# Two Gram matrices, an attention and 64 units on one core: turning x in 32x32 blocks on VectorE from quartered loads

## The chip, the core and the metric

One NeuronCore of a Trainium2 chip runs the kernel. TensorE (PE) multiplies matrices and writes to PSUM; VectorE (DVE), ScalarE (ACT) and GpSimd (POOL) compute elementwise; SyncE (SP) issues most DMAs. Each engine works through its own instructions strictly in order, and they meet through semaphores. The metric is the device time of the whole kernel in microseconds, from several runs, of which the median counts. All data is fp32.

## What is computed

x has the shape (16, 32, 128, 128). Two layers are added to it in turn, each fed with a group norm `_gn` of its input:

```python
x = x + _L0_conv_ref(_gn(x), Wq, Wkv, Wout, bout)
x = x + _L1_conv_ref(_gn(x), pn_g, pn_b, k1_..., k2_..., k3_..., k4_...)
```

Layer 0 is an attention between channels. The 16 images form two halves of 8 images x 32 channels = 256 rows of 16384 pixels each. q, k and v are linear in these rows, and the scores are summed over the pixels:

```python
sim = jnp.einsum('bin,bjn->bij', qh, kh) * scale
attn = jax.nn.softmax(sim, axis=-1)
out = jnp.einsum('bnj,bjd->bnd', attn, vh)
```

So for each half the scores follow from the 256x256 Gram matrix of the rows (x times x transposed, summed over 16384 pixels) and the row sums, and the whole layer becomes one 256x256 matrix that is applied to x. Layer 1 cuts the image into 8x8 windows and puts four small networks in each (`_fastkan`: a layer norm, eight Gaussians of each normalized value, a linear map of them, and a silu branch).

## The kernel before

The kernel has two stages: a head that makes the layer-0 matrix of each half, and a loop over 64 units (32 per half; a unit is 128 channels x 1024 pixels).

The head. `gram_load` fetches x in 32 loads of 1 MiB (128 partitions, rows of 4 KB) into three `u` tiles. `gram_turn` takes 512 pixels at a time: eight TensorE transposes (L616) into a PSUM tile `Y`, then one ScalarE copy (L624) into one of two `R` tiles, which puts the pixels on the partitions. `gram_sum` multiplies each step's 512 pixels with themselves in strips of 32 channels (L644), 64 matmuls a step, and sums 32 steps into one PSUM tile `X` for a half; only the strips on and above the diagonal blocks are computed. `attention(bp)` is a chain of some forty small steps that go to and fro between TensorE, VectorE and ScalarE, each through a `Y`: means, covariance (`rank_one` adds a rank-one matrix to the sum in `X` by L715; `gram_to` mirrors it), scores, softmax, the matrix `pts[bp]`, and the statistics for the second group norm. `X` is given back after the second `gram_to`. `projections` holds five tiles (two `z`, `ad_r`, two `u`) with the weights of layer 0 from the start until the second attention's end.

The loop. A unit passes through `load` (1 MiB of x, for two units), `layer0_norm` (L953 applies the matrix, L967 centres, L933 gets the variances), `keep`, `rows_norm` (L1000, L1005 to L1013), `move` (eight DMAs, L1046), `silus`, `norm_a` and `norm_b` (L415 into `Y`, L1063, L1066, L933 to L936, L1071), `scale_a`/`scale_b` (L1088), `seed_a`/`seed_b` (L1097 to L1105: four ScalarE activations into a `u` and two `R`), `ladder_a`/`ladder_b` (seven VectorE products each, L1117), `products_a`/`products_b` (L415 and L1153, L1272 into two `X`), `evict_a`, `move_back` (eight DMAs, L1189), `evict_z`, `result`, `again` and `store` (four DMAs of 32 partitions each, L1308).

The order. All tasks are Python generators that ask for steps (an engine, a length in us, tiles). `Flow.run` plans while the program is built: at each turn it picks, of the steps that could begin, the one that begins first by its own reckoning, and emits it. The order on each engine is thus fixed at build time; on the chip an engine waits at an instruction whose inputs aren't there. For the tasks of the loop the order on each engine is written out by hand in `ORDER` (task.step.behind: in slot m the unit m - behind), one period for a unit. Tasks that aren't named in it (the Gram tasks, projections, parameters and attention) go ahead of a named step on the same engine when they could begin no later. Tiles come from pools with a fixed number of buffers, and a step that finds none free can't be picked. Numbers of buffers that matter here: `Y` 2, `X` 2, `R` 3, `u` 6, `z` 2, `sz` 2, `yy` 2, `n` 2, `x`, `ad`, `ad_r` and `d` 1.

Of the kernel before, what the change touches and what calls it, by code (L numbers as in the profile page):

```python
# [46 lines left out]
LANDING = 2.5  # L47
BACK = 2
# [24 lines left out]
}  # L73
TURNS = 7
# [8 lines left out]
class Flow:  # L83
# [56 lines left out]
    def run(self, tasks, units):  # L140
# [32 lines left out]
        while True:  # L173
# [19 lines left out]
            found = []  # L193
            for engine, order in orders.items():
                while heads[engine] < len(order):
                    name, unit, k = order[heads[engine]]
                    x = where.get((name, unit))
                    if unit < 0 or unit >= units or (name, unit) in passed or (x is not None and x["at"][2] > k):
                        heads[engine] += 1
                        continue  # L200
                    break
                else:
                    continue
                head = next((c for c in able if c[1] is x and c[1]["at"][2] == k and c[1]["asks"][0] == engine), None)
                if head is not None:
                    found.append(head)
            free = [c for c in able if c[1]["at"][0] not in named]
            due = {c[1]["asks"][0]: c[0] for c in found}
            free = [c for c in free if c[0] <= due.get(c[1]["asks"][0], c[0])]
            for c in free:  # L210
                found = [d for d in found if d[1]["asks"][0] != c[1]["asks"][0]]
            at, x = min(found + free or able, key=lambda c: c[0])
# [7 lines left out]
def conv_preact_kernel(  # L220
# [34 lines left out]
    x_raw = x.rearrange("b c h w -> (b c) (h w)").rearrange("(k q p) n -> k p q n", q=KK, p=P)  # L255
    out_rows = out.rearrange("b c h w -> (b c) (h w)").rearrange(
# [166 lines left out]
    def layers():  # L423
        with ExitStack() as es:
# [12 lines left out]
                    "n": (sb, narrow, 2),  # L437
# [6 lines left out]
                    "ad": (sb, [P, 8, 2, P], 1),  # L444
                    "ad_r": (sb, [P, 8, 2, P], 1),
# [120 lines left out]
            NX = 3  # L566

            def projections():

                wq, wk, vo, low, mid = yield step("POOL", 5.0, "z", "z", "ad_r", "u", "u")  # L570
                vo = vo.rearrange("p l t w -> p (l t w)")
                wq = wq.rearrange("p (k n) -> p k n", k=KK)
                wk = wk.rearrange("p (k n) -> p k n", k=KK)
                wv_ = low[:, 0:1024].rearrange("p (h k c) -> p h k c", h=PAIRS, k=KK)
                wv_raw = vo[:, 0:1024].rearrange("p (h m s) -> p h m s", h=PAIRS * KK, s=2)
                wo = vo[:, 1024:2048].rearrange("p (h n) -> p h n", h=PAIRS)
# [9 lines left out]

            def gram_load():
                for m in range(NBP * NRB):
                    if m == 0:
                        xs = yield step("SP", 1.6, *["u"] * NX)  # L590
                    else:
                        if m >= NX:
                            yield "get", ("turned", 2 * (m - NX) + 1)
                        yield step("SP", 1.6)
                    bp, j = divmod(m, NRB)
                    t = xs[m % NX].rearrange("p (k n) -> p k n", k=KK)
                    nc.sync.dma_start(out=t, in_=x_raw[bp, :, :, j * RB : (j + 1) * RB])
                    put(("xs", m), t, fl.moved(2.6))

            STEPS = S // 512  # L600

            def gram_turn():
# [6 lines left out]
                for m in range(NBP * STEPS):  # L609
                    xr = yield "get", ("xs", m // 2)  # L610
                    o = (m % 2) * 512
                    tr, = yield step("PE", 0.95, "Y")
# [15 lines left out]
            def gram_sum():  # L628
# [5 lines left out]
                for m in range(NBP * STEPS):  # L634
                    bp, i = divmod(m, STEPS)
                    t = yield "get", ("xT", m)
                    for b in range(4):
                        got = yield step("PE", 0.55, *(["X"] if i == b == 0 else []), lag=0.0)
                        if got:
                            g = got[0]  # L640
# [796 lines left out]
```

## Time and profile before

| | us |
|---|---|
| median of 3 runs | 2930.34 (2930.0 to 2930.73) |
| the profiled execution | 2929.84 |
| its span, first to last instruction | 2927.8 |
| first Gram sum (L644) starts | 10.2 |
| first half's Gram matrix is read (L764) | 117.6 |
| second half's Gram matrix is read (L764) | 240.8 |
| first matmul of a unit's layer 0 (L953) | 240.6 |
| last step of the second attention (L921) | 300.3 |

The profile names engines by the abbreviations above (PEld is TensorE's loading of weights, which overlaps its matmuls), lines as L and a number, and tiles by their names without buffer numbers; a name can be that of the pool's tile, not of what lies in it, so that a line reading `u<-X` at L764 is the attention reading its Gram matrix. An fp32 matmul shows as two records. A time in front is us from the start of the span. The loads of x to the Gram stage are 32 of 1024 KB each, those of the loop another 32.

### The profile page before, as it was taken

To read this page: it belongs to the slowest core of one execution; us is meant where nothing else is said; L and a number is where in the kernel's file an instruction comes from. 1 tells how busy PE (TensorE), PEld (TensorE's weight loads), DVE (VectorE), ACT (ScalarE), POOL (GpSimd) and SP (SyncE) were. 2 spreads that over 40 slices of the span, in tenths; PEclk is the share of its full clock that TensorE was granted. 3 is DMA by queue.
4 is the path that set the end of the run, shared out by engine and by line. 5 is a ranking of instruction groups with operands and counts; after the bars stand their busy time and mean duration, and the time that the engine had idled before them with its cause. 6 is when DMAs were issued, how large, how long until landed. Compare 5 with 4: busy or idle time off the path is not lost.

```text
span 2927.8 us, 105440 instructions
## 1 busy us (share of the span) xinstructions
PE 2808.8 (96%) x48543; PEld 1138.2 (39%) x48543; DVE 2596.7 (89%) x1669; ACT 2578.1 (88%) x2089; POOL 53.6 (2%) x109
## 2 busy tenths in 40 slices
PE   8998899999999999999999999999999999999975
PEld 7885233333333333333333333333333333333321
DVE  1112699999999999999999999999999999999986
ACT  2222899999999999999999999999999999999973
POOL 7000000000000000000000000000000000000000
PEclk9998799999999999999999999999999999999998
DMA  6541223333433333443334343333344333334311
GB/s 206 172 126 63 58 72 112 103 109 112 116 106 107 108 105 113 113 113 91 110 103 109 113 115 110 103 112 105 111 113 114 96 104 105 108 113 114 97 56 39
DMA packets 196440, 311.33 MB, mean 106 GB/s; under 512 B 22944, under 2 KB 154528, under 8 KB 196000
## 3 DMA queue, kind: packets, MB, share of 16 engines
q1 hardware_dynamic: 192000, 302.07, 36.0%
q8 instruction: 382, 6.26, 0.9%
q0 software_dynamic: 3712, 2.46, 0.4%
q14 instruction: 58, 0.48, 0.1%
q10 hardware_dynamic: 288, 0.07, 0.0%
HBM read 103.18 MB, written 67.11 MB: 58 GB/s over the span
## 4 chain that ended last, share of the span: by engine, by line
PE 68%; DVE 21%; issue 6%; ACT 3%; DMA 1%; DVEq 0%; ACTq 0%; SPq 0%
PE X L415 24%; DVE u L1117 15%; PE X L1153 10%; PE Y L953 8%; PE X L644 5%; PE Y L415 4%; PE Y L967 4%; PE X L1272 4%; DVE yc L1088 3%; DVE yy L1005 2%; PE Y L933 2%; PE Y L616 2%; PE Y L1071 2%; ACT R L1099 0%; ACT u L1097 0%
## 5 line engine op out<-in xcount | busy, mean ns | idle before, releaser
L1117 DVE SCALAR_TENSOR_TENSOR u<-R,u 128x2048 f32<-128x2048 f32 x910 | 2042.5, 2286 | 33.8 <-ACT u L1102 17.0
L415 PE MATMUL X<-u,wt_a 32*32 32x512 f32 x16384 | 658.0, 601 | 8.7 <-ACT u L1102 4.2
L415 PE MATMUL X<-u,wt_b 32*32 32x512 f32 x16896 | 635.9, 602 | 18.2 <-ACT u L1102 9.3
L415 PEld LDWEIGHTS X<-u,wt_a 32*32 32x32 f32 x16384 | 302.8, 103 | 285.1 <-issue 134.4
L415 PEld LDWEIGHTS X<-u,wt_b 32*32 32x32 f32 x16896 | 224.5, 103 | 385.8 <-issue 196.5
L1088 DVE TENSOR_TENSOR yc<-yc,Y 128x1024 f32<-128x1024 f32 x260 | 305.4, 1216 | 13.1 <-PE Y L1071 9.8
L1097 ACT ACTIVATE u<-yc,vec 128x2048 f32<-128x2048 f32 x130 | 258.5, 1988 | 25.8 <-DVE yc L1088 21.2
L953 PE MATMUL Y<-x,pt 128*128 128x512 f32 x512 | 240.4, 613 | 34.0 <-DVE yc L1088 33.2
L1105 ACT ACTIVATE R<-yc,vec 128x2048 f32<-128x2048 f32 x130 | 259.5, 1996 | 2.1 <-DVE u L1117 1.2
L1099 ACT ACTIVATE R<-yc,vec 128x2048 f32<-128x2048 f32 x130 | 258.7, 1990 | 0.0
L1063 ACT ACTIVATE yc<-Y 128x1024 f32<-128x1024 f32 x260 | 250.4, 1017 | 8.3 <-PE Y L415 8.3
L1066 ACT ACTIVATE u<-yc 128x2048 f32<-128x2048 f32 x130 | 247.6, 1905 | 3.3 <-DVE u L1117 2.5
L1102 ACT ACTIVATE u<-u 128x2048 f32<-128x2048 f32 x130 | 247.1, 1901 | 0.0
L624 ACT COPY R<-Y 128x1024 f32<-128x1024 f32 x64 | 64.9, 1013 | 161.4 <-PE X L644 151.2
L935 ACT ACTIVATE lr<-Y,vec 128x512 f32<-128x512 f32 (+1 forms) x194 | 131.5, 678 | 39.0 <-PE Y L933 38.9
L953 PEld LDWEIGHTS Y<-x,pt 128*128 128x128 f32 x512 | 93.4, 192 | 184.4 <-issue 94.0
L644 PE MATMUL X<-R 128*32 128x161 f32 (+7 forms) x4096 | 146.0, 291 | 3.5 <-issue 3.4
L933 PE MATMUL Y<-u,e 128*32 128x512 f32 x1040 | 141.2, 608 | 5.0 <-ACT u L1066 5.0
L644 PEld LDWEIGHTS X<-R 128*32 128x32 f32 x4096 | 127.9, 110 | 24.5 <-issue 17.0
L1181 ACT ACTIVATE ad<-X,col 128x1024 f32<-128x1024 f32 x128 | 134.1, 1097 | 0.0
L967 PE MATMUL Y<-xh,c 128*128 128x512 f32 x256 | 128.8, 626 | 2.5 <-DVE yc L1088 1.4
L936 ACT ACTIVATE lr<-lr 128x512 f32<-128x512 f32 (+1 forms) x194 | 122.4, 631 | 6.2
(197 smaller groups left out, 2644.7 us busy)
## 6 DMA issues: line engine op xcount, KB each, us to landing
xh<-xh SPq DMA_DIRECT2D x128, 512.0 KB
d<-yy SPq DMA_DIRECT2D x512, 128.0 KB
ad_r<-ad SPq DMA_DIRECT2D x512, 128.0 KB
u<-in_x SPq DMA_DIRECT2D x32, 1024.0 KB
x<-in_x SPq DMA_DIRECT2D x32, 1024.0 KB
out<-xh SPq DMA_DIRECT2D x256, 128.0 KB
col<-in_cols POOLq DMA_DIRECT2D x32, 0.5 KB, 4.8
sz<-in_w POOLq DMA_DIRECT2D x32, 4.5 KB, 4.7
```

The costliest lines, as they stand in the source:

```text
L415: MM(dst(to, g_), lhsT=wt[32 * g_ : 32 * g_ + 32, :], rhs=rhs(g_, (to - turn[g_]) % 4), start=start, stop=stop,)
L644: MM(g[32 * q : 32 * q + 32, k, lo:hi], lhsT=t[:, b, at : at + 32], rhs=t[:, b, lo:hi], start=first, stop=last,)
L953: MM(xp[:, u, :], lhsT=pts[bp][:, k, kk * P : (kk + 1) * P], rhs=xr[:, k, u * 512 : (u + 1) * 512], start=k == 0, stop=k == KK - 1,)
L1063: ACT(v[:, i * RB : (i + 1) * RB], flat(yt[i]), AF.Identity)
L1066: ACT(sq, v, AF.Square)
L1088: TT(v[:, o], v[:, o], flat(rb[i]), ALU.mult)
L1097: ACT(u, v, AF.Square, bias=bq)
L1099: ACT(up, v, AF.Exp, bias=bp_, scale=2.0)
L1102: ACT(u, u, AF.Exp, scale=-1.0)
L1105: ACT(down, v, AF.Exp, bias=bn, scale=-2.0)
L1117: STT(t, by, BIG, tiles[at[way]], ALU.min, ALU.mult)
L1153: MM(dst(i, f), lhsT=wt(i)[o, o], rhs=rhs(i, o), start=False, stop=False)
```

## The change

- **Loads.** x comes to the Gram stage in 16 loads of 2 MiB (2048 pixels of 256 rows), each in eight DMAs: for each of two blocks of 128 rows and each quarter of the pixels, 32 channels go to 32 partitions, with four images side by side on a partition, in rows of 2 KB. The two buffers are made of `ad`, a `yy` and two `u` instead of three `u`. A load waits until the one two before has been turned.
- **Turning.** Two VectorE transposes (128x512, in 32x32 blocks) replace eight TensorE transposes and the ScalarE copy of a step. Because each quarter of the pixels lies on its own 32 partitions, the blocks need not cross them, and the result has pixels on partitions and the channels in order. The pixels of a step differ from before, the sum over them doesn't. The step no longer takes a `Y`.
- **The Gram matrix.** The PSUM tile is set to zero first. The attention copies the three blocks that it needs to SBUF and gives `X` back at once. `rank_one` writes its matrix to a `Y`, and VectorE adds it to the copy.
- **Where weights lie.** `projections` takes `ad_r`, one `z`, one `sz`, a new tile `att` and one `u`; `ad_r` is given back after the second attention's scores, the rest at its end. `n` has one buffer, `att` takes its room.
- **The planner.** Until the second Gram matrix is found, units 0 and 1 alone may be planned, and their steps in `ORDER` are searched past those of later units. Of two steps that could begin at the same time on an engine, units 0 and 1 go before the Gram tasks, not before attention, projections and parameters. A task that isn't named can't take a kind of tile for which a named step at the head of its order has waited 3 us or more.

```diff
+PATIENCE = 3.0
...
+FIRST = {"attention", "projections", "parameters"}
+AHEAD, UNTIL = 2, ("gram", 1)
...
-            found = []
+
+            found, kept = [], []
+            first = AHEAD if UNTIL not in self.found else units
             for engine, order in orders.items():
-                while heads[engine] < len(order):
-                    name, unit, k = order[heads[engine]]
+                i = heads[engine]
+                while i < len(order):
+                    name, unit, k = order[i]
                     x = where.get((name, unit))
-                    if unit < 0 or unit >= units or (name, unit) in passed or (x is not None and x["at"][2] > k):
+                    gone = not 0 <= unit < units or (name, unit) in passed or (x is not None and x["at"][2] > k)
+                    if gone and i == heads[engine]:
                         heads[engine] += 1
-                        continue
-                    break
+                    if not gone and unit < first:
+                        break
+                    i += 1
                 else:
                     continue
-                head = next((c for c in able if c[1] is x and c[1]["at"][2] == k and c[1]["asks"][0] == engine), None)
-                if head is not None:
-                    found.append(head)
-            free = [c for c in able if c[1]["at"][0] not in named]
-            due = {c[1]["asks"][0]: c[0] for c in found}
-            free = [c for c in free if c[0] <= due.get(c[1]["asks"][0], c[0])]
-            for c in free:
-                found = [d for d in found if d[1]["asks"][0] != c[1]["asks"][0]]
-            at, x = min(found + free or able, key=lambda c: c[0])
+                if x is None or x["at"][2] != k or x["asks"][0] != engine:
+                    continue
+                take = x["asks"][2]
+                at = self.start(x["time"], x["asks"])
+                if at is not None:
+                    found.append((at, x))
+                for kind in set(take):
+                    if all(len(self.free[o]) >= take.count(o) for o in take if o != kind):
+                        kept.append((x["time"], kind))
+            due = {c[1]["asks"][0]: (c[0], c[1]["at"][1]) for c in found}
+            others = []
+            for c in able:
+                name, engine = c[1]["at"][0], c[1]["asks"][0]
+                at, unit = due.get(engine, (c[0] + 1, 0))
+                late = c[0] > at or (c[0] == at and unit < AHEAD and name not in FIRST)
+                if name in named or late or any(t + PATIENCE <= c[0] and kind in c[1]["asks"][2] for t, kind in kept):
+                    continue
+                others.append(c)
+                found = [d for d in found if d[1]["asks"][0] != engine]
+            at, x = min(found + others or able, key=lambda c: c[0])
...
+    x_groups = x.rearrange("b c h w -> (b c) (h w)").rearrange("(n k g c) s -> n k c g s", k=KK, g=4, c=32)
...
-                    "n": (sb, narrow, 2),
+                    "n": (sb, narrow, 1),
...
+                    "att": (sb, narrow, 1),
...
-                wq, wk, vo, low, mid = yield step("POOL", 5.0, "z", "z", "ad_r", "u", "u")
-                vo = vo.rearrange("p l t w -> p (l t w)")
-                wq = wq.rearrange("p (k n) -> p k n", k=KK)
-                wk = wk.rearrange("p (k n) -> p k n", k=KK)
-                wv_ = low[:, 0:1024].rearrange("p (h k c) -> p h k c", h=PAIRS, k=KK)
-                wv_raw = vo[:, 0:1024].rearrange("p (h m s) -> p h m s", h=PAIRS * KK, s=2)
-                wo = vo[:, 1024:2048].rearrange("p (h n) -> p h n", h=PAIRS)
+                qk, wv_raw, wo, low, mid = yield step("POOL", 5.0, "ad_r", "z", "sz", "att", "u")
...
+            LOAD = 2048
+            STEPS = S // 512
+
             def gram_load():
-                for m in range(NBP * NRB):
+
+
+                for m in range(NBP * S // LOAD):
                     if m == 0:
-                        xs = yield step("SP", 1.6, *["u"] * NX)
+                        ad, yy, u0, u1 = yield step("SP", 5.2, "ad", "yy", "u", "u")
+                        flat4 = lambda t: t.rearrange("p l t w -> p (l t w)")
+                        xs = [
+                            [t.rearrange("p (g n) -> p g n", g=4) for t in pair]
+                            for pair in ((flat4(ad), flat4(yy)), (u0, u1))
+                        ]
                     else:
-                        if m >= NX:
-                            yield "get", ("turned", 2 * (m - NX) + 1)
-                        yield step("SP", 1.6)
-                    bp, j = divmod(m, NRB)
-                    t = xs[m % NX].rearrange("p (k n) -> p k n", k=KK)
-                    nc.sync.dma_start(out=t, in_=x_raw[bp, :, :, j * RB : (j + 1) * RB])
-                    put(("xs", m), t, fl.moved(2.6))
-
-            STEPS = S // 512
+                        if m >= 2:
+                            yield "get", ("turned", 4 * (m - 2) + 3)
+                        yield step("SP", 5.2)
+                    bp, j = divmod(m, S // LOAD)
+                    for r in range(4):
+                        for k in range(KK):
+                            at = j * LOAD + r * 512
+                            nc.sync.dma_start(
+                                out=xs[m % 2][k][32 * r : 32 * r + 32],
+                                in_=x_groups[bp, k, :, :, at : at + 512],
+                            )
+                    put(("xs", m), xs[m % 2], fl.moved(9.5, 4.5))
 
             def gram_turn():
 
@@ -607,23 +640,18 @@
                 for t in turned:
...
-                    xr = yield "get", ("xs", m // 2)
-                    o = (m % 2) * 512
-                    tr, = yield step("PE", 0.95, "Y")
-                    tr = tr.rearrange("p u (c k n) -> p (u c) k n", c=2, k=KK)
-                    for b in range(4):
-                        for k in range(KK):
-                            nc.tensor.transpose(
-                                tr[:, b, k, :], xr[:, k, o + b * P : o + (b + 1) * P], ident
-                            )
-                    put(("turned", m), None)
+                    xr = yield "get", ("xs", m // 4)
                     if m >= 2:
                         yield "get", ("summed", m - 2)
-                    yield step("ACT", 1.05)
-                    t = turned[m % 2]
-                    nc.scalar.copy(t.rearrange("p b (k n) -> p b k n", k=KK)[:, :, :, 0:P], tr)
-                    give("Y")
-                    put(("xT", m), t)
+                    yield step("DVE", 1.3)
+                    o = slice(128 * (m % 4), 128 * (m % 4) + 128)
+                    for k in range(KK):
+                        at = k * (P + 1)
+                        nc.vector.transpose(
+                            turned[m % 2][:, :, at : at + P].rearrange("p b (g c) -> p g b c", g=4), xr[k][:, :, o]
+                        )
+                    put(("turned", m), None)
+                    put(("xT", m), turned[m % 2])
...
-                        got = yield step("PE", 0.55, *(["X"] if i == b == 0 else []), lag=0.0)
-                        if got:
-                            g = got[0]
+                        if i == b == 0:
+                            g, = yield step("DVE", 1.1, "X")
+                            nc.vector.memset(g, 0.0)
+                        yield step("PE", 0.57, lag=0.0)
...
-                for kind in ["R"] * 2 + ["u"] * NX:
+                for kind in ("R", "R", "u", "u", "yy", "ad"):
...
-                    yield step("PE", 1.3)
-                    for k, c in ((0, 0), (0, 1), (1, 1)):
+                    ps_, = yield step("PE", 0.9, "Y")
+                    for k in range(KK):
                         MM(
-                            g[:, k, c * (P + 1) : c * (P + 1) + P],
+                            ps_[:, k, k * P : KK * P],
                             lhsT=scaled[:, k * P : (k + 1) * P],
-                            rhs=row[:, c * P : (c + 1) * P],
-                            start=False,
+                            rhs=row[:, k * P : KK * P],
+                            start=True,
                             stop=True,
-                            skip_group_check=True,
                         )
+                    yield step("DVE", 0.7)
+                    for k in range(KK):
+                        o = slice(k * P, KK * P)
+                        TT(g[:, k, o], g[:, k, o], ps_[:, k, o], ALU.add)
+                    give("Y")
 
                 def gram_to(dst, r):
...
-                yield step("DVE", 0.4)
+                yield step("ACT", 0.35, lag=0.0)
+                nc.scalar.copy(g[:, 0, P:], g_[:, 0, P + 1 : 2 * P + 1])
+                yield step("DVE", 0.6)
+                nc.vector.tensor_copy(g[:, 0, 0:P], g_[:, 0, 0:P])
+                nc.vector.tensor_copy(g[:, 1, P:], g_[:, 1, P + 1 : 2 * P + 1])
                 for k in range(KK):
-                    TS(mx[:, k : k + 1], g[:, k, P : P + 1], 1.0 / S, None, ALU.mult)
+                    TS(mx[:, k : k + 1], g_[:, k, P : P + 1], 1.0 / S, None, ALU.mult)
+                give("X", LAG)
...
-                give("X")
...
+                if bp == NBP - 1:
+                    give("ad_r")
...
-                    for kind in ("z", "z", "ad_r", "u", "u"):
+                    for kind in ("z", "sz", "att", "u"):
...
-            def load(m):
-                bp, kk, j = units[2 * m]
+            def load(n):
+
+                if n % 2:
+                    return
+                bp, kk, j = units[n]
...
-                        (("load", 2 * m, load(m)) for m in range(N // 2)),
+                        every("load", load),
```

## The prediction

> **What bounds the kernel now.** I first read the page's shares and its 40 slices, for where an engine is full and where not.
>
> ```profile
> PE 2808.8 (96%) x48543; PEld 1138.2 (39%) x48543; DVE 2596.7 (89%) x1669; ACT 2578.1 (88%) x2089; POOL 53.6 (2%) x109
> ...
> PE   8998899999999999999999999999999999999975
> ...
> DVE  1112699999999999999999999999999999999986
> ```
>
> From the sixth slice on (73 us each) TensorE and VectorE are full; before it VectorE is nearly idle. So there is a head stage, and behind it a loop that only more or less work can change. The busy time by windows, edges set at the stages, gives their sizes (columns: window, its us, then PE, PEld, DVE, ACT, POOL busy with counts, clock, DMA share, GB/s):
>
> ```profile
> 118.00:178.00 60.00, 60.00 (x990) 51.13 (x982) 16.87 (x74) 14.14 (x20) 0.00 (x0) 0.97 0.35 107
> 178.00:241.00 63.00, 62.10 (x1442) 55.35 (x1443) 0.45 (x4) 19.23 (x19) 0.00 (x0) 1.00 0.39 119
> 241.00:302.00 61.00, 46.26 (x222) 26.58 (x220) 19.46 (x79) 9.13 (x15) 0.00 (x0) 0.80 0.19 61
> 302.00:329.00 27.00, 19.25 (x96) 5.32 (x83) 7.43 (x8) 24.66 (x22) 0.00 (x0) 0.69 0.20 59
> ...
> 1000.00:1396.00 396.00, 390.67 (x6721) 142.10 (x6721) 392.49 (x221) 386.25 (x311) 0.00 (x0) 1.00 0.39 108
> ```
>
> Up to 241 us TensorE is the bound: the Gram sums, with the first half's attention beside them from 118 to 178. From 241 to 302 the second half's attention runs as a chain of small steps, from 302 to 329 the rest of the first unit's normalization: 88 us with no engine full. Then all three engines are 98 to 99% busy, ten units in 396 us. The timeline shows one Gram step and the first ladder products (start, length, engine, line):
>
> ```profile
> 225.60 1.09 PE L616 MATMUL Y<-ident,u 128*128 128x128 f32 x8
> 226.62 2.18 PE L644 MATMUL X<-R 128*32 128x257 f32 x64
> 227.46 1.01 ACT L624 COPY R<-Y 128x1024 f32<-128x1024 f32 x1 [2.12 <-PE X L644]
> 228.73 1.09 PE L616 MATMUL Y<-ident,u 128*128 128x128 f32 x8
> ...
> 328.77 22.48 DVE L1117 SCALAR_TENSOR_TENSOR u<-R,u 128x2048 f32<-128x2048 f32 x10
> ```
>
> A step of 512 pixels takes 228.73 - 225.60 = 3.13 us of TensorE: 1.02 to turn x, 2.11 to sum. The copy waits for TensorE, not the reverse. 64 steps are 200 of the 234 us up to 241. The ladder starts at 328.8, and 2927.8 - 328.8 = 2599 us follow.
>
> Last, the transfers: GB/s in 40 slices of 4 to 16 us (128-partition loads) and of 449 to 465 us (32-partition stores).
>
> ```profile
> GB/s 300 355 410 423 396 363 404 441 398 384 384 438 398 412 438 411 410 369 328 423 423 423 437 398 397 383 425 412 439 411 411 411 370 396 397 412 410 410 437 307
> ```
>
> ```profile
> GB/s 0 0 0 0 0 41 41 20 20 31 41 20 51 41 61 82 61 41 61 41 61 51 51 61 41 61 41 61 51 92 61 41 61 41 0 0 0 174 195 184
> ```
>
> A 32-partition transfer can thus be eight times slower than a full one, which matters below.
>
> [...] No row of the trace is a full-rate 32-partition load. [...] the trace has no transpose on VectorE.
>
> **The change part by part.** I sum against the profiled span, 2927.8 us (its run took 2929.8, the median is 2930.3).
>
> *Turning x.* TensorE loses 64 x 1.02 = 65 us, ScalarE its 64 copies of 1.01 us (idle there, worth nothing). VectorE gains 128 transposes of 128x512. Nearest row: the 128x512 copy out of PSUM, 0.691 us (L835). From 0.54 us (512 x 1.045 ns, the slope between L1088's 1216 ns for 1024 elements and L1117's 2286 for 2048, with no fixed cost) to 1.4 us (two passes of 0.691). I take 0.69: 1.4 us a step, hidden behind the 2.11 us of sums. At 1.4 us it would be 2.8 a step and bound the stage, 64 x 0.7 = 45 us late; only from 2.1 us is all gained lost.
>
> *Quartered loads.* 16 loads of 2 MiB, each 8 DMAs to 32 partitions in rows of 2 KB. [...] the best, if neighbouring quarters overlap, is the 5.2 us that 400 GB/s gives. I take 9.6. Four sums need 8.4 us, so loads are 1.2 us late each where TensorE has nothing else: the first half, 8 x 1.2 = 10 us. SP issues 128 DMAs where 32 were; eight (L1046 at 259.7) take it 5.2 us, 83 us in all over some 200. A load waits for the transposes of the one two before, and what SP holds behind it (keep, move, x) waits too: the first unit's move can lose one issue and one load, up to 15 us.
>
> *Gram copied out of PSUM.* Per half one 128x1024 memset (1.2 us, by L1088), three 128x128 copies (0.3 each, L743), and rank-one sums that go through Y and an add: 2 x about 2 us more on the chain. X returns right after the copy, not 27 us later. I take +4 us on each attention chain.
>
> *Units 0 and 1 beside the second half.* Turning no longer uses Y, so units and attention share it. But the turned tiles keep two of three R until the last sum, and a seed needs two: seeds stop before their last activation, and products wait for X. Only normalization moves forward.
>
> When does the last sum end? First load: 0.8 + 9.6 + 3.2 (5.8 us of the old first load less 2.6 for its 1 MiB at 400 GB/s) = 13.6, plus one turn 1.4 = 15. Sums 64 x 2.11 = 135. First attention on TensorE: 728 sum matmuls in 118 to 178 are 11.4 steps, 35.6 us, so 24. Weights 4. Units 0 and 1: L953 3.7, L967 2.0, L933 1.1, L1000 1.1 each, 16; unit 0's two norms 6. Loads late 10. Sum 210. The chain agrees: first Gram matrix 15 + 32 x 2.11 + 10 + 4 = 96; attention 60 as before, 4 for the copy, 2 for transposes in its way: 162; from there to a ladder 38 us by the lengths of 240.6 to 262 and 300 to 329 without the gaps, 55 with SP late: 200 to 217. I take the ladder at 212: 117 us earlier.
>
> What comes back: the second attention lies in a full loop. Its TensorE share is 24 us; VectorE's 17 fit beside. Unit 2's layer0 starts only after the last sum: 4 us. Unit 0's products stand behind it on TensorE, and it behind the load of x: 5.8 + 3.7 + 1.2 + 2.0 = 13 us, of which three ladder steps (6.9) cover half: 6. The attention keeps one u of six, one z, one sz, and ad_r until its scores; and its small VectorE steps queue behind 2.3 us ladder steps while Y is held, so that TensorE waits: 0 to 30, I take 8. Sum 42.
>
> n with one buffer costs nothing: it is used for 3 us once in 39.6. After the second attention the order is the old one, so the loop's 2599 us stay.
>
> 2927.8 - 117 + 42 = 2852.8; with the 2 us around the span, 2855.
>
> **Rivals.**
> - *All hides*: loads at 5.2 us, no late move, attention without stalls: ladder at 199, back 24 + 4 + 3: 2831. For: clock and TensorE have no gap there. [...]
> - *The attention stalls the loop*: unit 0's second z is needed about 90 us after the sums, and if the attention lasts longer everything behind that copy on ScalarE waits; +35: 2890. For: 241 to 302 already took 61 us nearly alone. Against: a wait of over 3 us outranks it.
> - *The units don't begin early* (the change doesn't do what it says): Y or yy held, so that normalization falls behind the sums. Sums end at 210 - 22 = 188, and the 88 us follow: ladder 276, 2877.
> - *The other side, slower: the quartered loads starve the head.* If 32-partition loads run as the 32-partition stores do, at 50 GB/s, 2 MiB take 42 us and 16 loads 671: the ladder some 480 us later than forecast, about 3330. It decides from 125 GB/s (16.8 us a load), where the 75 us are gone. For: the stores. [...]
>
> **How the numbers follow.** Forecast 0.57, all hides 0.15, stalled loop 0.11, no early units 0.09, starved head 0.06, slow transposes 0.02. The likeliest gives 2855; its own range is 2835 to 2878. To leave out 2 in 10 and hold the unknown costs ([...] stalls 0 to 30) the range is 2815 to 2897. About 0.2%, 6 us, is what this kernel's measurement can tell from no change: faster 0.91, same 0.01, slower 0.08.
>
> **What would show it.** L616 and the copies gone; a DVE transpose of about 0.69 us, 128 times; sums at 2.11 us pitch when no load is late; [...] layer0 (L953's matmuls) before the last sum; the first long row of ladder steps near 212 us; ten units in 396 us later. Wrong if transposes take over 1 us, if load slices lie below 150 GB/s, or if the stage after the last sum shows more than 50 us of TensorE idle or attention.

## The result, and the profile after

The median of five runs is 2920.1 us (2911.0 to 2920.8), against 2930.0 before (2926.8 to 2930.7). The ratio is 0.9961, with a 95% interval of 0.995 to 0.9972: a gain of about 10 us where 75 were forecast. The profiled execution has a span of 2918.5 us, 9.3 less than before.

The changed kernel's page, first the busy times, then the slices of 73 us for TensorE and VectorE, and the GB/s:

```profile
PE 2756.7 (94%) x48023; PEld 1091.7 (37%) x48023; DVE 2689.5 (92%) x1811; ACT 2515.1 (86%) x2027; POOL 53.6 (2%) x109
...
PE   5698899999999999999999999999999999999985
...
DVE  4455699999999999999999999999999999999986
...
GB/s 169 172 153 89 52 95 97 103 111 102 116 113 116 98 114 100 114 113 103 99 111 100 113 114 114 102 111 104 109 114 111 93 108 101 112 114 114 99 56 37
```

TensorE is busy 52 us less, VectorE 93 more, as intended. But the first two digits of TensorE fell from 8 and 9 to 5 and 6: the engine that was to be relieved now waits. From the fifth slice on the digits of both kernels are nearly the same. A unit of the loop still takes 39.6 us, since in ten units TensorE is as full as before (last line of the next two blocks).

Busy time by stretch, before (window, its us, then PE, PEld, DVE, ACT, POOL with counts, TensorE's clock, DMA share, GB/s):

```profile
0.00:100.00 100.00, 90.32 (x1939) 79.05 (x1939) 11.42 (x87) 29.67 (x29) 53.61 (x109) 1.00 0.68 208
100.00:210.00 110.00, 109.46 (x2116) 95.07 (x2107) 17.32 (x78) 29.71 (x35) 0.00 (x0) 0.98 0.44 135
210.00:340.00 130.00, 106.75 (x1226) 63.42 (x1230) 38.02 (x94) 53.83 (x53) 0.00 (x0) 0.83 0.19 58
340.00:420.00 80.00, 79.04 (x1376) 28.57 (x1369) 79.04 (x45) 77.91 (x62) 0.00 (x0) 1.00 0.31 81
1100.00:1496.00 396.00, 390.62 (x6722) 141.86 (x6720) 392.88 (x221) 386.51 (x311) 0.00 (x0) 1.00 0.39 108
```

The same stretches of the changed kernel:

```profile
0.00:100.00 100.00, 55.62 (x1373) 51.33 (x1375) 42.85 (x133) 1.28 (x1) 53.60 (x109) 0.86 0.84 174
100.00:210.00 110.00, 95.18 (x2136) 82.97 (x2130) 62.14 (x149) 2.68 (x9) 0.00 (x0) 0.94 0.75 153
210.00:340.00 130.00, 110.49 (x1618) 57.79 (x1618) 79.21 (x101) 74.63 (x66) 0.00 (x0) 0.91 0.32 78
340.00:420.00 80.00, 78.21 (x1258) 32.65 (x1258) 68.23 (x72) 63.39 (x55) 0.00 (x0) 0.97 0.26 74
1100.00:1496.00 396.00, 390.85 (x6720) 141.84 (x6716) 392.64 (x221) 386.06 (x311) 0.00 (x0) 1.00 0.37 108
```

The account is kept with TensorE's idle time, window length less PE busy. Before it is 9.7 + 0.5 + 23.3 + 1.0 = 34 us up to 420; after, 44.4 + 14.8 + 19.5 + 1.8 = 80.5 us. The change takes 65 us of turning from TensorE and adds 46 us of idling to it; that leaves 19. A part of the rest goes with the clock column: 0.86 where it was 1.00, and a record of the sums takes 311 ns on the mean of the Gram stage where it took 291. Of the 46 us, 35 lie in the first 100 and 14 in the next 110, and a little is regained later: TensorE's loss is in the Gram stage, not in the second attention or the loop.

Key times, from the lines of each kernel (start in us from the span's start; "given back" is the span after the first ladder product less the 2599.0 us of before). Forecast spans are the sums of the prediction's terms; "four buffers" and "no early units" are the experiments e4 and e10 below:

| | before | forecast | after | four buffers (e4) | four buffers, no early units (e10) |
|---|---|---|---|---|---|
| first Gram sum | 10.2 | 15 | 21.6 | 16.4 | 12.0 |
| first Gram matrix read | 117.6 | 96 | 134.6 | 112.2 | 106.0 |
| first layer-0 matmul of a unit | 240.6 | 162 | 209.7 | 182.1 | 202.1 |
| second Gram matrix read | 240.8 | 210 | 259.5 | 228.2 | 203.0 |
| first ladder product | 328.8 | 212 | 273.6 | 237.8 | 264.9 |
| given back | - | 42 | 45.9 | 44.3 | 18.5 |
| span | 2927.8 | 2853 | 2918.5 | 2881.1 | 2882.4 |

So the ladder starts 55 us earlier, not 117, and 46 of the 55 are given back, nearly the 42 of the forecast. The miss of 62 us in the ladder's start begins with the first Gram matrix (39 us late), and attention and first normalization add 9 and 14.

VectorE, which now turns x, has these waits in the changed kernel (start, length, instruction; in brackets the idle time before it and its releaser):

```profile
17.26 0.71 DVE L650 STREAM_TRANSPOSE R<-ad 128x512 f32<-128x512 f32 x1 [9.74 <-DMA ad<-in_x]
...
20.64 0.91 DVE L668 MEMSET X<- 128x1024 f32 x1 [0.21 <-issue]
...
41.48 0.71 DVE L650 STREAM_TRANSPOSE R<-ad 128x512 f32<-128x512 f32 x1 [3.70 <-DMA ad<-in_x]
...
68.25 0.31 DVE L550 TENSOR_TENSOR sz<-sz,fac 128x144 f32<-128x144 f32 x1 [3.08 <-DMA wt_b<-in_w]
...
84.52 0.46 DVE L572 TENSOR_TENSOR wt_b<-wt_b,fac 128x288 f32<-128x288 f32 x1 [13.08 <-DMA sz<-in_w]
...
106.39 0.71 DVE L650 STREAM_TRANSPOSE R<-ad 128x512 f32<-128x512 f32 x1 [1.95 <-DMA ad<-in_x]
```

The transpose takes 0.71 us. Its inputs are late (9.74 at the first load, then 3.70 and 1.95), and VectorE also stands for 13.08 and 3.08 us at instructions that prepare layer-1 weights, which GpSimd fetches with small DMAs (2 to 18 KB); the transposes behind them wait too. After the first sum and up to the first Gram matrix its waits for loads of x add up to 9.5 us, those for weights to 16.2. The loads are issued by SP in groups of eight DMAs (the `ad` groups continue as single rows, left out):

```profile
9.26 9.27 SPq L629 DMA_DIRECT2D u<-in_x  x8
29.04 0.31 SPq L629 DMA_DIRECT2D ad<-in_x  x1
...
36.99 5.85 SPq L629 DMA_DIRECT2D u<-in_x  x8
54.67 0.31 SPq L629 DMA_DIRECT2D ad<-in_x  x1
...
94.14 0.31 SPq L629 DMA_DIRECT2D ad<-in_x  x1
...
117.97 0.32 SPq L629 DMA_DIRECT2D ad<-in_x  x1
```

Each pair of buffers comes round in 24 to 39 us. Eight loads have been issued before the ninth at 117.97: 14.6 us a load, where four steps of sums need 8.4. In a stretch with the DMA engines full of loads of x the rate is 205 GB/s (the window 108 to 112 below; the 207 GB/s at 88 to 92 are weights for the attention, which GpSimd fetches), which makes 10.2 us for 2 MiB. The 9.6 us of the forecast were the author's assumption, for the trace of before has no load of x to 32 partitions. But over the first 100 us only 174 GB/s flow. Between the loads lies the wait for a buffer, in SP's queue (engine, line, what it waited for, total us, times, longest):

```profile
SPq L629 <- DVE R L650: 138.5, 25, 19.4
SPq L1232 <- PE Y L845: 58.9, 1, 58.9
```

The second line is `move_back` of the first unit, held until the second attention gives `ad_r` back; it is tried in e6.

So far the loads look guilty by being late. TensorE's own gaps say something else. These are the sums of the first half that follow a gap (left out are the very first and a last one of 1.71 us):

```profile
42.59 5.83 PE L673 MATMUL X<-R 128*32 128x33 f32 x128 [3.16 <-issue]
51.80 5.93 PE L673 MATMUL X<-R 128*32 128x33 f32 x97 [3.38 <-issue]
67.10 6.91 PE L673 MATMUL X<-R 128*32 128x65 f32 x164 [3.24 <-issue]
86.95 13.36 PE L673 MATMUL X<-R 128*32 128x257 f32 x348 [12.94 <-DVE R L650]
101.64 4.21 PE L673 MATMUL X<-R 128*32 128x65 f32 x128 [1.33 <-issue]
107.83 5.86 PE L673 MATMUL X<-R 128*32 128x65 f32 x128 [1.99 <-issue]
115.95 8.21 PE L673 MATMUL X<-R 128*32 128x65 f32 x256 [2.25 <-issue]
125.60 4.21 PE L673 MATMUL X<-R 128*32 128x65 f32 x128 [1.44 <-issue]
```

Only one gap, 12.94 us, ends with a turned tile, and that tile stood behind the wait for a weight. Eight gaps, 18.5 us together, are put down to "issue": the profile shows nothing that ended them. They lie in the middle of a step, whose tile had been turned as a whole before the step began, so that a late tile can't have ended them. What the trace has there is packets of 16 KB in the DMA queue that the page lists as "q8 instruction". In all eight cases one of them ended 1.4 to 1.6 us before TensorE went on, and in the loop one such packet goes with some 254 of TensorE's records, half of them matmuls and half weight loads (53 packets from 1100 to 1496). From 20 to 135 us a packet takes 1.36 us in the median, in the kernel before 1.00. So it looks as if TensorE waited for its own instructions, whose packets go slower among these loads. That is the author's estimate from the trace; no run tests it by itself.

Last, TensorE's clock in three stretches of 4 us:

```profile
52.00:56.00 4.00, 4.00 (x70) 3.55 (x66) 1.54 (x3) 0.00 (x0) 3.51 (x8) 0.50 0.14 24
88.00:92.00 4.00, 4.00 (x79) 3.59 (x73) 1.61 (x3) 0.00 (x0) 0.00 (x0) 0.55 1.00 207
108.00:112.00 4.00, 4.00 (x86) 3.72 (x84) 1.98 (x3) 0.00 (x0) 0.00 (x0) 0.59 1.06 205
```

Here TensorE has 70 to 86 matmul records in 4 us, at a clock of 0.50 to 0.59. From 28 to 36, 92 to 100 and 116 to 124 us, at a clock of 1.00, it has 132 to 139 in the same time. Each of the three stretches follows a gap of TensorE (3.4, 12.9 and 2.0 us). In these places a gap is thus paid for twice, by itself and by slower sums behind it.

### The profile page after: what moved, and what is told of

Its sections match the earlier page's. It is cut to its first block, busy times and chain, and to the rows that moved or that the text cites. A ratio compares the mean times of both kernels' runs of the same rounds, so it can differ in the third digit from the quotient of the medians.

```text
span 2918.5 us, 104813 instructions
## 1 busy us (share of the span) xinstructions
PE 2756.7 (94%) x48023; PEld 1091.7 (37%) x48023; DVE 2689.5 (92%) x1811; ACT 2515.1 (86%) x2027; POOL 53.6 (2%) x109
## 4 chain that ended last, share of the span: by engine, by line
PE 62%; DVE 20%; issue 6%; ACT 5%; DMA 4%; SPq 1%; POOL 1%; DVEq 0%; ACTq 0%; POOLq 0%
PE X L436 24%; DVE u L1160 15%; PE X L1196 9%; PE Y L996 7%; PE Y L1010 4%; PE Y L436 4%; PE X L1315 4%; PE X L673 3%; DVE yc L1131 3%; PE Y L1114 2%; PE Y L973 2%; DVE yy L1048 2%; DMA sz<-in_w 1%; SPq L1232 1%; DMA col<-in_cols 1%
## 5 line engine op out<-in xcount | busy, mean ns | idle before, releaser
L1148 ACT ACTIVATE R<-yc,vec 128x2048 f32<-128x2048 f32 x130 | 259.5, 1996 | 3.0 <-DVE u L1160 2.1
L673 PE MATMUL X<-R 128*32 128x161 f32 (+7 forms) x4096 | 156.1, 311 | 61.0 <-issue 25.5
L673 PEld LDWEIGHTS X<-R 128*32 128x32 f32 x4096 | 141.2, 118 | 81.4 <-issue 33.1
L975 ACT ACTIVATE lr<-Y,vec 128x512 f32<-128x512 f32 (+1 forms) x194 | 131.3, 677 | 46.8 <-PE Y L973 46.8
L996 PEld LDWEIGHTS Y<-x,pt 128*128 128x128 f32 x512 | 92.6, 191 | 182.1 <-issue 93.7
L1196 PE MATMUL X<-sd,silu_a 64*64 64x512 f32 x1024 | 124.7, 602 | 0.0
```

The lines of the kernel that those rows point to most:

```text
L673: MM(g[32 * q : 32 * q + 32, k, lo:hi], lhsT=t[:, b, at : at + 32], rhs=t[:, b, lo:hi], start=first, stop=last,)
L996: MM(xp[:, u, :], lhsT=pts[bp][:, k, kk * P : (kk + 1) * P], rhs=xr[:, k, u * 512 : (u + 1) * 512], start=k == 0, stop=k == KK - 1,)
L1148: ACT(down, v, AF.Exp, bias=bn, scale=-2.0)
L1196: MM(dst(i, f), lhsT=wt(i)[o, o], rhs=rhs(i, o), start=False, stop=False)
```

## The experiments

After the result the suspects were: weights that stand before transposes in VectorE's order; the loads, by their rate to 32 partitions or by the wait for a buffer; the early units, which might buy nothing; and the wait for `ad_r`. All kernels except e5 keep VectorE's turning. Ratios are against the kernel before.

**e1: the layer-1 weights' steps planned 45 us later.**

```diff
-raw, = yield step("POOL", 40.0, "sz")
+raw, = yield step("POOL", 40.0, "sz", lag=45.0)
```

> The changed kernel with one number changed: the planner is told that the loads of layer 1's weights are there 45 us later, so that VectorE's steps on them stand some 40 us later in its order, behind more transposes. Theory A (the head is late because its new waits stand in a row, and what is late there is late at the end): VectorE no longer waits 13.1 + 3.1 us for a weight with transposes queued behind it, the first Gram matrix is read at about 118 us instead of 134, and the time falls by 10 to 18 us, to 2902 to 2910. Theory B (what sets the end is the chain after the last sum, where the second attention meets the units): the Gram matrix comes earlier, but the time stays within 5 us of 2920.

Measured: 2917.3 us (2913.2 to 2921.2), ratio 0.9962 (0.9947 to 0.9977), no gain over the change itself. The waits for weights are gone from the first 100 us, and the first Gram matrix is read at 128.1 instead of 134.6. TensorE's gaps put down to "issue" grow from 18.5 to 26.3 us there, so another wait took the place of part of this one. And the first attention ends at 208.3 as before (209.0): 20 steps of sums (1280 matmuls) stand beside it in TensorE's order in both, and it lasts 80.2 us instead of 74.4. Why wasn't taken apart; VectorE waits for no load in that stretch.

**e2: no early units.**

```diff
-AHEAD, UNTIL = 2, ("gram", 1)
+AHEAD, UNTIL = 0, ("gram", 1)
```

> The changed kernel with AHEAD = 0: no unit may begin before the second Gram matrix is found. Theory A: the last sum ends some 20 us earlier (about 235 us instead of 257), but layer 0 of unit 0 starts there instead of at 210, the ladder starts at about 300 to 315 instead of 274, and with part of the second attention before it the time is 2930 to 2945. Theory B (the early start is taken back by the second attention among the units anyway): within 5 us of 2920.

Measured: 2920.4 us (2915.4 to 2925.1), ratio 0.9973 (0.9964 to 0.9981), not to be told from the change. The last sum starts 13 us earlier (243.9 for 256.7), the ladder 33 later (306.5), and 17.5 us are given back instead of 45.9. What the early units win at the ladder's start they lose behind it.

**e3: full loads.** Two DMAs of 128 partitions a load, with the same two buffers.

```diff
-for r in range(4):
-    for k in range(KK):
...
-            out=xs[m % 2][k][32 * r : 32 * r + 32],
-            in_=x_groups[bp, k, :, :, at : at + 512],
+for k in range(KK):
...
+        out=xs[m % 2][k].rearrange("p g n -> p (g n)"),
+        in_=x_raw[bp, :, k, j * LOAD : (j + 1) * LOAD],
```

> The changed kernel with each 2 MiB load made of two DMAs of 128 partitions in rows of 8 KB instead of eight of 32 partitions in rows of 2 KB. The pixels and channels then lie elsewhere, so what is summed is not the Gram matrix; instructions and bytes are the same. It prices the 32-partition loads. Theory A: 2 MiB land in 5 to 6 us instead of 10, the first sum starts at about 13 us instead of 21.6, no transpose waits for a load afterwards, TensorE's clock stays near 1.0 between 95 and 135 us, the first Gram matrix is read at about 105 us and the time falls by 20 to 30 us. Theory B: within 5 us of 2920.

Measured: 2889.5 us (2888.0 to 2890.4), ratio 0.9867 (0.9852 to 0.9881): 28 us better than the change by the ratios, 31 by the medians. The first Gram matrix is read at 111.6. The wait for buffers in SP's queue, in this kernel:

```profile
SPq L627 <- DVE R L648: 161.8, 25, 20.0
```

SP waits longer for buffers than in the changed kernel (161.8 for 138.5 us), yet after the first load and up to the first Gram matrix no transpose waits for x: a fast load that begins late still ends in time. So a wait in SP's queue isn't a loss by itself.

This edit changes the loads' DMAs alone; the other engines' steps and their order stay. So these 28 to 31 us are the price of the change's loads (32 partitions, eight DMAs a load, rows of 2 KB). The first sum starts 6 us earlier, the second half gains 11, and between the first sum and the first Gram matrix 16.6 us go: TensorE's gaps put down to "issue" fall from 18.5 to 9.0 us, and the 2048 matmul records of the sums take 72.3 us instead of 79.1. The gap behind the weights stays (10.9 us).

**e5: the loads and the TensorE turning of before, all else as changed.**

```diff
-LOAD = 2048
...
+NX = 3
+def gram_load():
...
+                nc.tensor.transpose(
+                    tr[:, b, k, :], xr[:, k, o + b * P : o + (b + 1) * P], ident
+                )
...
+        nc.scalar.copy(t.rearrange("p b (k n) -> p b k n", k=KK)[:, :, :, 0:P], tr)
```

> The changed kernel with the loads and the turning of the kernel before (32 loads of 1 MiB to 128 partitions into three u, eight TensorE transposes and a ScalarE copy a step); the Gram matrix copied out of PSUM, the new places of the weights and the early units stay. Theory A: a step takes 3.13 us of TensorE again, the first Gram matrix is read at about 118 us (before: 117.6), layer 0 of unit 0 starts at about 185 instead of 210, the last sum ends at about 262, the ladder starts at about 265, and the time is about 2910: the turning on VectorE brought nothing, the early units all. If VectorE's turning is what gains and the early units are not: about 2930 or more.

Measured: 2922.5 us (2919.6 to 2925.0), ratio 0.9975 (0.9967 to 0.9983). TensorE idles 31.6 us up to 420, hardly less than before. The other parts of the change are thus worth 7 us without the new turning, and the turning on VectorE with its loads, the centre of the change, adds only 2 to 4 us as it stands (by the medians and by the ratios).

**e4: four buffers of 1 MiB in place of two of 2 MiB, in the same tiles.** Rows are 1 KB instead of 2.

```diff
-LOAD = 2048
+LOAD, NX = 1024, 4
-xs = [[... for t in pair] for pair in ((flat4(ad), flat4(yy)), (u0, u1))]
+xs = [t.rearrange("p (k g n) -> p k g n", k=KK, g=4) for t in (flat4(ad), flat4(yy), u0, u1)]
-if m >= 2: yield "get", ("turned", 4 * (m - 2) + 3)
+if m >= NX: yield "get", ("turned", 2 * (m - NX) + 1)
```

> The changed kernel with the loads cut in half: 32 loads of 1 MiB (1024 pixels, rows of 1 KB, still eight DMAs to 32 partitions each) into four buffers made of the same tiles; a buffer is loaded again after two steps, not four. Theory C (a late load is mostly the wait for its buffer: two loads take 24 us between 94 and 142 us where the bytes alone need 20 at 207 GB/s, and TensorE's clock then falls for some us): transfers run without pauses, 2 MiB take 10 to 11 us, the first Gram matrix is read at about 115 us instead of 134.6, the last sum ends at 235 to 245, and the time falls by 10 to 20 us. Theory D (the rate to 32 partitions alone is the limit, and shorter rows make it worse): first Gram matrix at 130 us or later, time 2915 to 2935.

Measured: 2882.4 us (2879.2 to 2884.3), ratio 0.984 (0.9825 to 0.9855), 35 us better than the change by the ratios, 38 by the medians. The stretches and the buffer wait of e4:

```profile
0.00:100.00 100.00, 65.84 (x1777) 60.35 (x1780) 51.95 (x146) 1.28 (x1) 53.77 (x109) 0.93 1.08 212
100.00:210.00 110.00, 104.27 (x2179) 84.38 (x2175) 63.26 (x150) 10.96 (x18) 0.00 (x0) 0.97 0.83 177
210.00:340.00 130.00, 115.55 (x1729) 55.85 (x1720) 93.23 (x131) 87.95 (x80) 0.00 (x0) 0.92 0.16 47
340.00:420.00 80.00, 77.98 (x1340) 28.11 (x1344) 79.02 (x47) 76.41 (x62) 0.00 (x0) 1.00 0.33 95
```

```profile
SPq L626 <- DVE R L647: 28.1, 20, 5.8
```

The same bytes go by DMAs to 32 partitions as in the change, yet 212 GB/s flow where 174 did, and SP waits 28.1 us for buffers where it waited 138.5. TensorE's idle time falls by 24 us to 56 (10 in the first 100 us, 9 in the next); up to the first Gram matrix its gaps put down to "issue" fall from 18.5 to 6.8 us. The account closes to within 4 us: 65 of turning less 22 of idling more than before is 43, and the span is 46.7 shorter than before. The number of buffers, the length of the rows and, with them, the planned order changed together, so the run doesn't show which of them did it.

**e6: the weights of q and k in a `z` and an `sz`, so that `ad_r` isn't held by the attention.**

```diff
-qk, wv_raw, wo, low, mid = yield step("POOL", 5.0, "ad_r", "z", "sz", "att", "u")
+wq, wk, wv_raw, wo, low, mid = yield step("POOL", 5.0, "z", "sz", "z", "sz", "att", "u")
```

> The changed kernel with the weights for q and k in a z and a sz instead of ad_r (both given back after the second attention's scores, as ad_r was), so that move_back of unit 0 needn't wait for them. Theory A2 (the hole of VectorE from 330 to 348 us is unit 0's move_back, which waited 58.9 us for ad_r, and behind it products_b of unit 0 on TensorE): no such wait on SP, no hole, and the time falls by 12 to 18 us, to 2902 to 2908. Theory B2 (the hole is the second attention's own chain, which fills TensorE there): within 5 us of 2920.

Measured: 2916.2 us (2914.2 to 2924.6), ratio 0.9959 (0.9946 to 0.9972). The 58.9 us wait is gone. The second attention now ends at 386 instead of 376, and ScalarE waits 11.7 us at `evict_z` for TensorE (until 330 us), where it waited 12.0 in the changed kernel (until 349): the loop is held up as before, without the wait for `ad_r`. No clear gain.

**e9: half of each load's DMAs issued by ScalarE, two buffers as in the change.**

```diff
-nc.sync.dma_start(out=xs[m % 2][k][32 * r : 32 * r + 32],
+(nc.scalar if r > 1 else nc.sync).dma_start(out=xs[m % 2][k][32 * r : 32 * r + 32],
```

> The changed kernel with the DMAs of the last two quarters of each load (partitions 64 to 127) issued by ScalarE, those of the first two by SP, so that transfers to both halves of the partitions can be under way together. [...] slices of up to 300 to 400 GB/s, 2 MiB in 6 to 7 us, first Gram matrix at about 110 us, time 2890 to 2900, close to the run with 128-partition loads. If queues don't overlap so: about 207 GB/s, time within 6 us of 2920.

Measured: 2912.7 us (2909.4 to 2916.4), ratio 0.9944 (0.9928 to 0.9961), 5 us below the change by the ratios and 7 by the medians, with ranges that overlap. The transfers did get faster (222 GB/s from 8 to 20 us, where the changed kernel has 206 from 6 to 16; over the first 100 us 185 where it has 174), and after the first load VectorE waits only 2.1 us for x, where it waited 9.5. Still the first Gram matrix is read at 131.3, not at 110. With the order of steps unchanged, this speaks against late tiles as the cause: they are nearly gone here, the time is not. What stays is TensorE's gaps put down to "issue" (19.1 us) and the slow sums (78.3 us).

**e8: the edits of e1, e4 and e6 together.**

> Three edits together: four buffers of 1 MiB, VectorE's steps on the weights 45 us later in the plan, and q's and k's weights in a z and a sz. If theories A, A2 and C hold and the gains add up: first Gram matrix at about 105 us, no hole after the last sum, time 2880 to 2895. If only one of them holds: 2900 to 2912. If none: 2915 to 2925.

Measured: 2882.5 us (2881.2 to 2887.1), ratio 0.9844 (0.983 to 0.9859): no more than e4 alone. The last sum comes at 210, 17 us earlier than in e4, but the ladder at 261.5 instead of 237.8. The first half's sums end at 105, as hoped, but the Gram matrix is read only at 129.8: VectorE's copy of it stands behind transposes of the second half in the planned order. So the run took the wait for weights away and put another delay in its place.

**e10: e4 without early units** (e2's edit on top).

> Four 1 MiB buffers as in e4, but no unit begins before the second Gram matrix is found. With the loads as the change has them the early units bought nothing (2920.4 without, 2917 to 2920 with). If early units are worth their normalization (unit 0's and 1's layer-0, rows and moves, some 22 us of TensorE that otherwise stand in the hole after the last sum) once no load is late, this is 15 to 25 us slower than e4: about 2897 to 2907, with the last sum near 212 instead of 227 and the ladder near 275. If the two things trade evenly as they do with late loads, it equals e4 within 3 us: 2879 to 2885.

Measured: 2883.9 us (2878.9 to 2885.8), ratio 0.9838 (0.9821 to 0.9856). Its stretches:

```profile
0.00:100.00 100.00, 70.03 (x1950) 64.02 (x1953) 55.81 (x151) 1.28 (x1) 54.04 (x109) 0.95 1.06 205
100.00:210.00 110.00, 102.84 (x2332) 88.43 (x2321) 65.35 (x158) 5.03 (x12) 0.00 (x0) 0.97 0.78 162
210.00:340.00 130.00, 114.17 (x1398) 47.95 (x1402) 88.70 (x121) 93.66 (x86) 0.00 (x0) 0.91 0.23 66
340.00:420.00 80.00, 78.72 (x1371) 28.35 (x1372) 79.02 (x45) 77.62 (x62) 0.00 (x0) 1.00 0.33 96
```

The ladder starts at 264.9 instead of 237.8, and by 420 both have done 53 of its steps. Early units win 27 us at the ladder's start and give 26 back. TensorE's idle time is 54 us in e10 and 56 in e4: they change where it works, not how much it idles. This was so with the loads of the change (e2) and is so with those of e4.

**e11: e4 and two queues together.**

```diff
-nc.sync.dma_start(out=xs[m % NX][32 * r : 32 * r + 32, k],
+(nc.scalar if r > 1 else nc.sync).dma_start(out=xs[m % NX][32 * r : 32 * r + 32, k],
```

> Four 1 MiB buffers as in e4, and half of each load's DMAs (the upper two quarters of the partitions) issued by ScalarE. If after e4 the loads are still late by their rate (about 207 GB/s, 5.1 us for 1 MiB against 4.2 us that two steps of sums need), the two queues at 250 or more bring 4.1 us a load and the last sum comes up to 10 us earlier: 2870 to 2876. If the rate no longer matters, 2880 to 2885. If ScalarE's part of the attention is held up by its waits for buffers, the first attention ends later than 181 and the time is over 2888.

Measured: 2884.2 us (2879.3 to 2887.2), ratio 0.9838 (0.9821 to 0.9856), the same as e4. The first Gram matrix is read 7 us earlier (105.4), but the last sum starts at 227.4 as in e4 (227.0). So with four buffers the rate of the loads isn't what sets the end.

## Why the prediction was wrong

- *What held*: the direction, and what moves. Turning left TensorE and ScalarE, a transpose took 0.71 us (0.69 forecast), units began before the last sum, and ten units still take 396 us.
- *What is given back*: 42 forecast, 45.9 measured. As a sum this held, but by luck, since its parts didn't. It was charged mostly to the second attention; e2 and e10 give back 17.5 and 18.5 without early units, so that some 27 us belong to the early units and cancel their gain.
- *The step that failed: "Loads late 10. Sum 210."* This was the only thing that the sum let hold TensorE up in the first half, apart from 4 us of weights: 32 steps of 2.11 us and 10 us of late loads, 78 in all. They took 134.6 - 21.6 = 113 us. The lateness itself is about as large as forecast: a load takes 10.2 us for 9.6, and VectorE waits 9.5 us for x after the first load. But of TensorE's 113 us, 79.1 are sums (67.5 forecast), 12.9 lie behind the wait for a weight, and 18.5 are gaps that no late tile ended. A buffer's round, 14.6 us a load, doesn't explain this either: the buffers come free late because the turns wait for TensorE (29.0 us up to there), and e3 keeps the two buffers and waits longer for them without harm.
- *What is shown of the cause*: that the loads cost it. e3 changes their DMAs alone and takes 16.6 us out of the 113 and about 30 from the time; e4, with smaller loads, takes 17.2 and some 35. Not by late tiles, since e9 removes most of those and gains 5 to 7 us. What goes with the time is TensorE's gaps put down to "issue", up to the first Gram matrix: 3.0 us in the kernel before, 18.5 in the change, 26.3 in e1, 19.1 in e9, but 9.0 in e3 and 6.8 in e4; and with them the time of the sums, 79.1, 78.6 and 78.3 us in the change, e1 and e9, but 72.3 and 74.4 in e3 and e4. That the gaps are waits for instructions behind the loads' packets is the author's estimate and wasn't tested; why fewer come with e4's loads is open.
- *Two costs not in the sum.* VectorE's wait for weights (16 us in the first 100) was missing, since before VectorE was idle there and nobody waited behind it. e1 shows that to take it away alone brings nothing. The clock is the other: the sums of the first half take longer where TensorE has more gaps (79.1 us at a mean clock of 0.89 in the change, 74.4 at 0.94 in e4). That is seen, not tested by itself.
- *First load, 15 forecast, 21.6 measured*: the first transpose waits until 17.3; then four transposes, two of them for the next step, and the clearing of `X` stand before the first sum.
- *The first attention, 66 forecast, 74 measured*: it carries 20 steps of sums on TensorE (1280 matmuls), where the kernel before had some 12 (756 recorded).
- *Rivals*: the slower one, a head starved by its loads, came in effect and not by its mechanism: at 205 GB/s the loads are far above the 125 below which it decides. A stalled loop can't be ruled out as a part: between 210 and 340 TensorE idles 19.5 us, less than the 23.3 of before, but between 340 and 420 VectorE and ScalarE are busy 11 and 15 us less than before. e6 took away one wait there without a clear gain. That units don't begin early wasn't what happened, but its 2877 is near the 2884 of e10, where they don't and the loads are e4's.

What stays open: e4's span is still 28 us above the forecast's, 16 of them lost by the first Gram matrix. There TensorE still has a gap of 9.7 us behind VectorE's wait for a weight. e8 removed that wait but read the Gram matrix later, and e11 came 7 us earlier without any gain at the end; what sets e4's end, TensorE's order among sums, attention and first units, wasn't taken apart further.

e4 beats both kernels: 2882.4 us, 1.6% below the kernel before; e8, e10 and e11 can't be told from it. Its simplest form is e10, with no early units at all.

## What to carry to other kernels

Before a late input is blamed, look at the gaps of the engine that bounds the stage and at what ended each. Here late tiles and long waits for buffers were easy to see, but a faster load (e9) removed most of the late tiles and gained 5 to 7 us, while gaps inside steps whose data was there went with the 30 us of e3. When work moves to an engine that was idle, look through that engine's order for instructions which wait for something else: what waited for free before is now ahead of the critical work. And sum up the bound engine's idle time before and after by stretch: work that starts earlier pays only if that sum falls.

## What the runs showed of the hardware

- DMAs to 32 partitions each, issued one after the other by SP to all four quarters, moved 205 to 208 GB/s with rows of 2 KB (changed kernel, 96 to 112, nothing else but instructions under way). With rows of 1 KB they moved 205 and 206 (e4, 20 to 32 and 32 to 44, beside GpSimd's small loads of weights). With the upper two quarters issued by ScalarE it was 222 in each of the same two windows (e11), and 257 and 255 from 68 to 80 and from 80 to 92, where e4 had 224 and 227.
- Behind gaps of 2.0, 3.4 and 12.9 us TensorE's clock was 0.50 to 0.59 in a stretch of 4 us (changed kernel), but not behind every gap: after the 2.25 us before 115.95 it was 1.00 from 116 to 124, and four steps ran in 8.2 us.
- In the changed kernel TensorE stood still eight times inside a step, 1.3 to 3.4 us each, and went on 1.4 to 1.6 us after a 16 KB packet of the instruction queue had ended. In the kernel before, with loads to 128 partitions, there were four such gaps, 3.0 us in all, up to the first Gram matrix.
